# Routing, shared experts and expert blocks of a Macaron layer: another order of the first routing, an earlier table of overflow blocks, and more buffers for results and their rows

## The chip, the cores and the metric

The kernel runs on one core of a Trainium2 chip. A core has five engines that work at the same time: TensorE (PE, matrix products and transposes), VectorE (DVE), ScalarE (ACT), GpSimd (POOL) and SyncE (SP, here only a queue of DMA issues). The metric is the device time of one execution in microseconds (us); the time of a kernel is the median of its runs.

## What is computed

A layer over 4096 tokens of 256 values, all in float32: half a feed-forward, attention, half the same feed-forward again.

```python
x = x + 0.5 * ffn(layernorm(x))
x = x + attention(layernorm(x))      # 16 heads of 16 values
x = x + 0.5 * ffn(layernorm(x))

def ffn(x):
    scores = softmax(x @ Wg)                      # 32 experts
    weights, indices = top_k(scores, 4)
    y = 0
    for e in range(32):                           # at most 2048 tokens each
        y[tok] += swiglu(x[tok], W1[e], W2[e], W3[e]) * w
    return y + swiglu(x, Ws1, Ws2, Ws3)           # the shared expert
```

## The kernel before

**Stages.** The program runs six stages one after the other: `first_front` (routing and shared expert of the first feed-forward), `Layer.experts` of layer 0, `projections` (sum of the expert results, then queries, keys and values), `attention` (into which routing and shared expert of the second feed-forward are woven), `Layer.experts` of layer 1, and a last loop that sums the results.

**Order.** Inside `tc.manual_schedule(engines=ORDERED)` PE, ACT, DVE and SP work their instructions in the order in which the program writes them; only POOL's order is chosen by the framework. The order around the change is thus written out by hand, with generators: each `yield` ends a piece, and the caller decides which piece comes next. A tile with `bufs=n` has n buffers in turn; who writes a buffer again waits until its last reader is done, and what is written behind the waiting instruction on the same engine waits too.

**Routing** (`route`, L201 to L357, in chunks of 8 x 128 tokens in layer 0 and 4 x 128 in layer 1). `normalize` takes statistics on DVE (L141, L142) and writes the rows into `xr` (on ACT at L163 in layer 0, on DVE at L167 in layer 1); `turned` transposes them (L177, L180). Then gate logits (L233), softmax and top-k on DVE (L243 to L257), one-hot masks (L262 to L267), positions by a product with a triangle of ones (L273), overflow arithmetic (L281 to L332), slots (L338 to L344), and 4 indirect DMAs per 128 tokens by POOL (L350) that scatter the rows with their tags to `xg` in DRAM. Columns D + K and up of `xr` hold for each of the 4 choices the row of `ys` that the result belongs to; L222 writes them, ahead of the statistics. `xr` has 3 buffers in layer 0, for 4 chunks.

Each expert owns 512 slots; tokens beyond these go to overflow blocks of 128 rows, of which 24 are always worked (a condition works more if there are more). Which expert owns an overflow block is worked out by `share_out` (L531 to L581): transposes of the running counts `given` (L558), member tables on DVE (L561 to L566), a product (L570), and from it `eb` (the expert) and `wrow` (the row of its weights, L578), by which POOL gathers weights (L663).

**Shared expert.** `shared_half` (L410 to L453) for layer 0, 8 halves of 512 tokens: first piece 16 products (L421) and tanh (L430); second piece the gate products on DVE (L436, L437); third piece 8 products (L443), the sum (L451) and a store by SP (L452). `shared` (L359 to L408) does the same for layer 1 in smaller pieces (L375, L384 to L389, L395, L403, store L408).

**`first_front`** (L774 to L860): for each of the 4 chunks the pieces of routing, and within chunks 1 to 3 one half of the shared expert. After the last routing come the five other halves, each half's third piece after the next one's second.

**Attention** (L1136 to L1298): scores (L1170), exponentials (L1180), values (L1188), division and projection; the pieces of `front(b)` (L1240 to L1254: `route`, then `shared`) are put between steps of the next block. For the last block no step is left, so its pieces are worked one after the other at the end. PSUM is given out by `Banks`: `Banks.tile` lends always the bank that is just not the accumulator, so two tiles in a row share one bank.

**Experts** (`experts`, L502 to L529): `share_out`, then `run_blocks` (L629 to L655) over 56 blocks, 32 of 512 rows (kind "expert") and 24 of 128 (kind "more"). In round n it loads weights of block n + 4 and rows of block n + 3, turns block n + 1 (`turn`: transposes L692, copies L696 and L698, and `toi`, the target rows of the result, L700 to L709), does the first half of block n (L718, silu L727, product `hT` L729) and the second half of block n - 1 (L740, copies to `yb` L744 and L746, and 4 or 1 indirect DMAs by POOL, L748, that send the rows of `yb` to the rows of `ys` that `toi` names). `toi` has 4 buffers and `yb` the pool's 3. On DVE a round is written in the order copy, `toi`, `hT`, `yb`.

The projections hold squares of queries and keys in `sq` (L938, 7 buffers), read by L947.

Of the kernel before, what the change touches and what calls it, by code (L numbers as in the profile page):

```python
# [9 lines left out]
F32 = mybir.dt.float32  # L10
I32 = mybir.dt.int32
# [7 lines left out]
P = 128  # L19
# [40 lines left out]
def kernel(  # L60
# [122 lines left out]
    class Layer:  # L183
# [17 lines left out]
        def route(self, ch, xt, pool, pm):  # L201
# [14 lines left out]
            def over_t(a):  # L216
# [4 lines left out]
            self.xT = xT  # L221
            nc.vector.tensor_scalar(  # L222
                xr[:, :, D + K :], iota_y[:, :n, :], float(t0 * P * KR), None, ALU.add
            )
            rows = [xr[:, i, 0:D] for i in range(n)]
# [27 lines left out]
            for t in range(n):  # L253
                nc.vector.max(top[:, t, :], sc[:, t, :])
                nc.vector.max_index(idx[:, t, :], top[:, t, :], sc[:, t, :])
            idxf = xr[:, :, D : D + K]
            nc.vector.tensor_copy(idxf, idx[:, :, 0:K])  # L257
# [244 lines left out]
        def experts(self, low=None):  # L502
            if low is not None:
                few = nc.values_load(low[0:1, 0:1], min_val=0, max_val=1)
                with tc.If(few > 0), tc.tile_pool(name="low", bufs=1) as pool:
                    self.clear_low(pool)
            with (
                tc.tile_pool(name=f"expert{self.index}", bufs=3, reuse_waits="tile") as pool,
                tc.tile_pool(name=f"ps_t{self.index}", bufs=2, space=PSUM) as ps_t,
                tc.tile_pool(name=f"ps_h{self.index}", bufs=4, space=PSUM) as ps_h,  # L510
                tc.tile_pool(name=f"ps_o{self.index}", bufs=2, space=PSUM) as ps_o,
            ):
                ps = (ps_t, ps_h, ps_o)
                self.wrow = pool.tile([P, NOVMAX], I32, name="wrow", bufs=1)
                self.eb = pool.tile([P, NOVMAX], F32, name="eb", bufs=1)
                more = pool.tile([P, 1], I32, name="more", bufs=1)
                with tc.manual_schedule(engines=ORDERED):
                    halves = self.share_out(pool, ps_t, more)
                    blocks = []
                    for e in range(E):  # L520
                        blocks.append(("expert", e))
                        blocks += [
                            ("more", b) for b in range(e * NOV // E, (e + 1) * NOV // E)
                        ]
                    self.run_blocks(blocks, pool, ps)
                    large = nc.values_load(more[0:1, 0:1], min_val=0, max_val=1)
                    with tc.If(large > 0):
                        self.clear_rest(pool, ps_t, halves)
                        self.run_blocks([("more", b) for b in range(NOV, NOVMAX)], pool, ps)  # L529

        def share_out(self, pool, ps_t, more):  # L531

            def tile(n, name, dtype=F32):
                return pool.tile([P, n], dtype, tag=name, name=name, bufs=1)

            nc.vector.tensor_scalar(more[:], self.total[:], float(NOV), None, ALU.is_gt)

            whole = tile(1, "whole", I32)  # L540
            nc.vector.tensor_copy(whole[:], iota_p[:])
            nc.vector.tensor_scalar(
                whole[:], whole[:], E.bit_length() - 1, None, ALU.arith_shift_right
            )
            mod = tile(1, "mod")
            nc.vector.tensor_copy(mod[:], whole[:])
            nc.vector.tensor_scalar(mod[:], mod[:], -float(E), iota_p[:], ALU.mult, ALU.add)
            expert_of = tile(P, "expert_of")
            nc.vector.tensor_scalar(expert_of[:], ones[:], mod[:], None, ALU.mult)

            halves = []
            nch = P // E
            for h in range(self.nch // nch):
                columns = tile(3, f"columns{h}")
                for i in range(3):
                    tp = ps_t.tile([P, P], F32, tag="tp", name="given_ps")
                    part = self.given[:, i, h * nch : (h + 1) * nch, :]
                    nc.tensor.transpose(tp[:], part.rearrange("p c e -> p (c e)"), ident[:])  # L558
                    nc.vector.tensor_copy(columns[:, i : i + 1], tp[:, 0:1])
                end = tile(1, f"end{h}")  # L560
                nc.vector.tensor_add(end[:], columns[:, 0:1], columns[:, 1:2])  # L561
                member = tile(NOVMAX, f"member{h}")
                inside = tile(NOVMAX, f"inside{h}")
                nc.vector.tensor_scalar(member[:], iota_b[:], columns[:, 0:1], None, ALU.is_ge)
                nc.vector.tensor_scalar(inside[:], iota_b[:], end[:], None, ALU.is_lt)
                nc.vector.tensor_mul(member[:], member[:], inside[:])  # L566
                halves.append((member, columns))
            ps = ps_t.tile([P, NOVMAX], F32, tag="tp", name="eb_ps")
            for h, (member, _) in enumerate(halves):
# [10 lines left out]
            )  # L580
            return halves  # L581

# [88 lines left out]
        def load_rows(self, kind, i, pool):  # L671
            if kind == "expert":
                n, r, e = S0 // P, i * S0, float(i)
            else:
# [3 lines left out]

            nc.sync.dma_start(
                xb[:], self.xg[r : r + n * P, :].rearrange("(p i) d -> p i d", p=P)  # L680
            )
            return {"n": n, "r": r, "e": e, "xb": xb}

        def turn(self, b, pool, ps_t):
# [19 lines left out]
            nc.vector.tensor_reduce(to[:, :n], pair[:, :n], AX.X, ALU.add)  # L704
            toi = pool.tile([P, S0 // P], I32, tag="toi", name="toi", bufs=4)
            slot = iota_s[:] if n > 1 else iota_p[:]
# [25 lines left out]
        def second_half(self, b, pool, ps_o):  # L732
            w2, hT, n = b["w"][:, 2 * NC * H :], b["hT"], b["n"]
            yb = pool.tile([P, S0 // P, D], F32, tag="yb", name="yb")
            group = f"send{self.index}"
# [38 lines left out]
    def first_front(layer, keep):  # L774
        n = layer.n
        with (
# [57 lines left out]

            half = halves()
            norm(0)
            go_on(0, turns)
            norm(1)
            for ch in range(nch):
                go_on(ch, 1)  # L840
                if ch + 1 < nch:
                    go_on(ch + 1, turns)
                go_on(ch, 2)
                between = next(half) if ch > 0 else iter(())
                next(between, None)
                go_on(ch, 3)
                next(between, None)
                if ch + 2 < nch:
                    norm(ch + 2)
                next(between, None)  # L850
            flag = layer.low(keep)

            late = iter(())
            for it in half:
                next(it)
                next(it)
                next(late, None)
                late = it
            next(late, None)
        return flag  # L860

    def projections(layer, side):
# [4 lines left out]
        with (  # L867
# [48 lines left out]
            def queries_or_keys(c, i, xT):  # L916

                squares = []
                for g in range(NG):
# [16 lines left out]
                    if i == 0:  # L936
                        nc.scalar.dma_start(qd[c, g], part)
                    sq = pool.tile([P, QB], F32, tag="sq", name="sq", bufs=2 * NG - 1)  # L938
                    nc.scalar.activation(sq[:], ps[:], AF.Square, bias=bias)
# [195 lines left out]

    def attention(layer, kT, v, shift):  # L1136

# [4 lines left out]
        with (  # L1142
# [97 lines left out]
            def front(b):  # L1240
# [8 lines left out]
                def both():  # L1249
                    xt = xs[b]  # L1250
                    yield from layer.route(b, xt, pool, pm)
                    yield from layer.shared(b, xt, layer.xT, pool, pm)

# [79 lines left out]
    with tc.tile_pool(name="keep0", bufs=1) as keep:  # L1333
# [5 lines left out]
        with tc.tile_pool(name="kv", bufs=1, side="right", reuse_waits="tile") as kv:  # L1339
# [6 lines left out]
            layer = Layer(1, side, QT, nc.vector.tensor_copy)  # L1346
            attention(layer, kT, v, shift)
    layer.experts()
# [75 lines left out]
```

## Time and profile before

| | us |
|---|---|
| median of 3 runs (lowest to highest) | 3372.26 (3371.22 to 3374.43) |
| the profiled execution | 3374.66 |
| its span (first to last instruction) | 3372.8 |
| first front, to the last DVE sum | 0 to 229.1 |
| experts of layer 0, PE's first to last product | 236.6 to 491.4 |
| sums and projections | 502 to 707 |
| attention with the second front | 707 to 3024 |
| experts of layer 1, PE's first to last product | 3033.6 to 3292.2 |
| last sums and stores | 3302 to 3372.8 |

In lines of the profile, PE is the matrix engine, PEld its weight loads, `DVEq`, `SPq` and the like an engine's queue. A line of the timeline has the start, the duration, engine and line of the program, the operation, what it writes and reads, how many are merged, and in brackets the idle time of the engine before it with what ended it. A line of waits has who waited for whom, then the sum in us, the number of times and the longest. The granted clock is the share of full speed that PE had.

### The profile page before, as it was taken

The page shows a single profiled execution, that of the slowest core. Times are in us where ns is not written, and L with a number is a line of the kernel's source. Part 1 is how long each engine was busy: PE and PEld are TensorE (multiplying, and loading weights), DVE is VectorE, ACT ScalarE, POOL GpSimd, SP SyncE. Part 2 cuts the span into 40 slices and gives each one's busy share as a digit, 9 for nine tenths or more (in the row PEclk, how much of TensorE's full clock was granted, in tenths as well). Part 3 has the DMA queues.
Part 4 walks back from the last instruction along what each step waited for, and adds up shares of the span by engine and source line. Part 5 has one row for each costly group of instructions (what it writes and reads, how often), then busy time and mean ns, then how long its engine had stood idle before and what let it go on. Part 6 is the DMA issues. An engine that isn't in the chain of part 4 may idle for free.

```text
span 3372.8 us, 50148 instructions
## 1 busy us (share of the span) xinstructions
PE 3072.7 (91%) x20183; PEld 1066.8 (32%) x20183; DVE 975.3 (29%) x2837; ACT 2334.9 (69%) x3753; POOL 616.0 (18%) x644
## 2 busy tenths in 40 slices
PE   4589977989999999999999999999999999959990
PEld 3356653422222222222222222222222222226660
DVE  6744437810112103201211210220121131044447
ACT  2112224569999898898999989889989998912220
POOL 2756661100001000100100010010010001025661
PEclk9799998989999999999999999999999999969995
DMA  6347756441300000000000010000000000017767
GB/s 236 118 182 244 247 189 242 153 135 56 100 4 20 26 7 4 27 20 4 30 20 4 13 33 4 7 27 20 4 30 20 4 6 31 1 64 238 254 204 315
DMA packets 130352, 282.20 MB, mean 84 GB/s; under 512 B 23472, under 2 KB 70192, under 8 KB 129712
## 3 DMA queue, kind: packets, MB, share of 16 engines
q1 hardware_dynamic: 82976, 165.84, 14.6%
q0 software_dynamic: 31872, 97.56, 7.9%
q10 hardware_dynamic: 15248, 15.38, 1.3%
q8 instruction: 163, 2.67, 0.3%
q14 instruction: 93, 0.76, 0.1%
HBM read 146.64 MB, written 132.06 MB: 83 GB/s over the span
## 4 chain that ended last, share of the span: by engine, by line
PE 70%; DVE 3%; issue 2%; DMA 2%; POOL 1%; ACT 0%; DVEq 0%; POOLq 0%; SPq 0%
PE banks L1170 33%; PE banks L1188 30%; PE banks L375 2%; DMA ys<-yb,toi 2%; PE h L718 2%; DVE xt L765 1%; POOL ys L748 1%; PE banks L1260 1%; PE banks L395 1%; PE o L740 1%; PE banks L233 1%; PE xbt_ps L692 0%; PE banks L177 0%; POOL wb L663 0%; DVE hT L729 0%
## 5 line engine op out<-in xcount | busy, mean ns | idle before, releaser
L1180 ACT ACTIVATE ex<-banks 128x512 f32<-128x512 f32 (+1 forms) x3223 | 2055.7, 714 | 164.7 <-PE banks L1170 129.1
L1170 PE MATMUL banks<-q,kT 32*128 32x512 f32 x8192 | 1177.6, 641 | 12.4 <-DVE q L1157 11.1
L1188 PE MATMUL banks<-ex,v 128*17 128x512 f32 x8192 | 1078.9, 598 | 0.0
L350 POOL DMA_INDIRECT xg<-xr,sidx x256 | 248.2, 969 | 2282.3 <-DVE beyond L343 2163.4
L1170 PEld LDWEIGHTS banks<-q,kT 32*128 32x128 f32 x8192 | 327.4, 183 | 847.4 <-ACT ex L1180 704.5
L1188 PEld LDWEIGHTS banks<-ex,v 128*17 128x17 f32 x8192 | 136.1, 95 | 777.5 <-issue 776.5
L1208 DVE COPY o<-banks 128x512 f32<-128x512 f32 x32 | 22.1, 691 | 1185.4 <-PE banks L1188 647.2
L748 POOL DMA_INDIRECT ys<-yb,toi x304 | 293.0, 964 | 177.3 <-DVE yb L746 94.8
L718 PE MATMUL h<-xT,w 128*128 128x512 f32 x512 | 236.0, 604 | 0.0
L744 ACT COPY yb<-o 128x512 f32<-128x512 f32 x64 | 37.5, 586 | 178.8 <-PE o L740 153.0
L740 PE MATMUL o<-w,hT 128*128 128x256 f32 x512 | 126.7, 392 | 34.2 <-DVE hT L729 34.2
L698 ACT COPY xT<-xbt_ps 128x512 f32<-128x512 f32 (+1 forms) x112 | 50.6, 452 | 126.4 <-PE xbt_ps L692 124.8
L727 ACT ACTIVATE s<-h 128x512 f32<-128x512 f32 (+1 forms) x112 | 51.5, 460 | 107.0 <-PE h L718 105.4
L718 PEld LDWEIGHTS h<-xT,w 128*128 128x128 f32 x512 | 95.2, 196 | 95.2 <-issue 95.2
L922 PE MATMUL qk_ps<-xT,wqk_sb 128*128 128x512 f32 x256 | 113.5, 602 | 1.7 <-ACT xT L180 1.7
L740 PEld LDWEIGHTS o<-w,hT 128*128 128x128 f32 x512 | 95.4, 194 | 55.1 <-DVE hT L729 36.9
L1211 DVE RECIPROCAL den<-den 128x512 f32<-128x512 f32 x32 | 107.3, 3353 | 1.1
L765 DVE SCALAR_TENSOR_TENSOR xt<-y,wk,xt 128x256 f32<-128x256 f32 x192 | 95.1, 495 | 6.9
L729 DVE TENSOR_TENSOR hT<-s,h 128x512 f32<-128x512 f32 (+1 forms) x112 | 57.8, 516 | 74.9 <-PE h L718 71.7
L375 PE MATMUL banks<-xT,ws_sb 128*128 128x512 f32 x128 | 68.9, 664 | 8.6 <-DVE u L385 6.5
L692 PE MATMUL xbt_ps<-ident,xb 128*128 128x128 f32 x512 | 69.6, 282 | 7.7 <-DMA xb<-xg 7.7
L443 PE MATMUL so<-ws_sb,shT 128*128 128x256 f32 x128 | 36.2, 441 | 43.5 <-DVE shT L437 28.9
(215 smaller groups left out, 1781.2 us busy)
## 6 DMA issues: line engine op xcount, KB each, us to landing
y<-ys SPq DMA_DIRECT2D x64, 640.0 KB, 6.9
xb<-xg SPq DMA_DIRECT2D x64, 528.0 KB, 5.7
w<-in_wexp_dram SPq DMA_DIRECT2D x64, 384.0 KB, 3.4
xg<-zeros SPq DMA_DIRECT2D x152, 132.0 KB, 2.3
xg<-zero SPq DMA_DIRECT2D x32, 264.0 KB, 4.3
qd<-q ACTq DMA_DIRECT2D x32, 256.0 KB, 5.5
q<-qd SPq DMA_DIRECT2D x32, 256.0 KB, 2.6
xbb<-xg SPq DMA_DIRECT2D x48, 132.0 KB, 3.7
```

The source lines that it names most:

```text
L350: ins = nc.gpsimd.indirect_dma_start(out=self.xg[:], out_offset=bass.IndirectOffsetOnAxis(ap=self.sidx[:, t0 + t, k : k + 1], axis=0), in_ ...
L375: nc.tensor.matmul(ps[:], ws13_sb[:, c, h0 : h0 + P], xT[:, c, i0 * P : (i0 + QT) * P], start=(c == 0), stop=(c == NC - 1),)
L692: nc.tensor.transpose(tp[:, i * P : (i + 1) * P], xb[:, i, c * P : (c + 1) * P], ident[:])
L718: nc.tensor.matmul(ps[:, : n * P], w[:, (j * NC + c) * H : (j * NC + c + 1) * H], xT[:, c, : n * P], start=(c == 0), stop=(c == NC - 1),)
L740: nc.tensor.matmul(o[:, i, :], hT[:, (i0 + i) * P : (i0 + i + 1) * P], w2, start=True, stop=True)
L748: ins = nc.gpsimd.indirect_dma_start(out=ys[:], out_offset=bass.IndirectOffsetOnAxis(ap=b["toi"][:, i : i + 1], axis=0), in_=yb[:, i, :], ...
L765: nc.vector.scalar_tensor_tensor(xt, y[:, k, :], self.wk[:, t, k : k + 1], y[:, K, :] if k == 0 else xt, ALU.mult, ALU.add,)
L922: nc.tensor.matmul(ps[:], wqk_sb[:, cc, (i * NG + g) * P : (i * NG + g + 1) * P], xT[:, cc, :], start=(cc == 0), stop=(cc == NC - 1),)
L1170: nc.tensor.matmul(pm.all[:, banks[j], :], kT[rows, g, t * P : (t + 1) * P], q[rows, :], start=True, stop=True,)
L1180: nc.scalar.activation(ex[:, i : i + n, :], pm.all[:, k : k + n, :], AF.Exp, scale=SCALE)
L1188: nc.tensor.matmul(acc[j * HP : j * HP + HV, :], v[:, t, g * HG + j, :], ex[:, j, :], start=(t == 0), stop=(t == NT - 1),)
L1211: nc.vector.reciprocal(den[:], den[:])
```

## The change

- `route` writes the constant columns of `xr` (L222) after the top-k instead of ahead of the statistics.
- `first_front` puts two halves of the shared expert into each of the chunks 1 to 3; the third piece of the second one waits in the list `late` and is worked in the next chunk, after the logits and the next chunk's transposes (`finish`). Two halves are left for the end.
- `share_out` is called at the end of `first_front`, ahead of these two halves, and in `attention` between `route` and `shared` of the last block, instead of at the start of `experts`. What must live on lies in the pools `keep0` and `side`, its PSUM tiles come from the front's pool or from `Banks`.
- The rows of the first expert block are loaded by four DMAs, one for each of the four rows of a partition.
- `toi` gets 12 buffers instead of 4, `yb` 6 instead of 3, `sq` 6 instead of 7.

```diff
@@ route
-            nc.vector.tensor_scalar(
-                xr[:, :, D + K :], iota_y[:, :n, :], float(t0 * P * KR), None, ALU.add
-            )
             rows = [xr[:, i, 0:D] for i in range(n)]
...
                 nc.vector.max_index(idx[:, t, :], top[:, t, :], sc[:, t, :])
+            nc.vector.tensor_scalar(
+                xr[:, :, D + K :], iota_y[:, :n, :], float(t0 * P * KR), None, ALU.add
+            )
@@ experts
-                    halves = self.share_out(pool, ps_t, more)
...
-        def share_out(self, pool, ps_t, more):
+        def share_out(self, pool, pm, scratch):
...
-                    tp = ps_t.tile([P, P], F32, tag="tp", name="given_ps")
+                    tp = pm.tile([P, P], F32, tag="m", name="given_ps")
...
-            ps = ps_t.tile([P, NOVMAX], F32, tag="tp", name="eb_ps")
+            ps = pm.tile([P, NOVMAX], F32, tag="m", name="eb_ps")
@@ load_rows
-            nc.sync.dma_start(
-                xb[:], self.xg[r : r + n * P, :].rearrange("(p i) d -> p i d", p=P)
-            )
+            parts = n if kind == "expert" and i == 0 else 1
+            rows = self.xg[r : r + n * P, :].rearrange("(p i) d -> p i d", p=P)
+            for a in range(0, n, n // parts):
+                part = slice(a, a + n // parts)
+                nc.sync.dma_start(xb[:, part, :], rows[:, part, :])
@@ turn
-            toi = pool.tile([P, S0 // P], I32, tag="toi", name="toi", bufs=4)
+            toi = pool.tile([P, S0 // P], I32, tag="toi", name="toi", bufs=12)
@@ second_half
-            yb = pool.tile([P, S0 // P, D], F32, tag="yb", name="yb")
+            yb = pool.tile([P, S0 // P, D], F32, tag="yb", name="yb", bufs=6)
@@ first_front
+            late = []
+
+            def finish():
+                while late:
+                    next(late.pop(0))
+
...
                     go_on(ch + 1, turns)
+                finish()
                 go_on(ch, 2)
-                between = next(half) if ch > 0 else iter(())
-                next(between, None)
+                one, two = (next(half), next(half)) if ch > 0 else (iter(()), iter(()))
+                next(one, None)
                 go_on(ch, 3)
-                next(between, None)
+                next(one, None)
+                next(two, None)
                 if ch + 2 < nch:
                     norm(ch + 2)
-                next(between, None)
+                next(one, None)
+                next(two, None)
+                if ch > 0:
+                    late.append(two)
             flag = layer.low(keep)
-
-            late = iter(())
+            layer.share_out(keep, pm, pool)
+
             for it in half:
                 next(it)
                 next(it)
-                next(late, None)
-                late = it
-            next(late, None)
+                finish()
+                late.append(it)
+            finish()
@@ projections
-                    sq = pool.tile([P, QB], F32, tag="sq", name="sq", bufs=2 * NG - 1)
+                    sq = pool.tile([P, QB], F32, tag="sq", name="sq", bufs=2 * NG - 2)
@@ attention
                     yield from layer.route(b, xt, pool, pm)
+                    if b == NQB - 1:
+                        layer.share_out(keep, pm, pool)
                     yield from layer.shared(b, xt, layer.xT, pool, pm)
```

## The prediction

> **What bounds the kernel now.** I read the page first: PE is busy 91% of the span, and in section 4 the chain is PE for 70%. But the two big PE lines (L1170, L1188) are the attention stage, which the change hardly touches, so I cut the span by stage with the table of stretches, and looked in each touched stage for the wait that ends last.
>
> ```profile
> PE 3072.7 (91%) x20183; PEld 1066.8 (32%) x20183; DVE 975.3 (29%) x2837; ACT 2334.9 (69%) x3753; POOL 616.0 (18%) x644
> ...
> 249.70:491.40 241.70, 224.33 (x1008) 153.12 (x1006) 101.71 (x320) 63.26 (x138) 160.12 (x167) 0.99 0.71 233
> 3047.60:3292.20 244.60, 227.72 (x1008) 155.33 (x1006) 101.72 (x320) 63.35 (x138) 159.35 (x166) 0.97 0.69 230
> 700.00:3000.00 2300.00, 2265.57 (x16971) 557.10 (x16972) 410.67 (x1065) 2067.98 (x3247) 108.34 (x113) 0.99 0.07 24
> ```
>
> Columns: stretch, its length, busy time of PE, PEld, DVE, ACT, POOL, granted clock, DMA share, GB/s. The first two stretches are the two expert stages from the moment their pipelines run to PE's last matmul. PE is idle there for 17.4 and 16.9 us. The waits of these stages (windows 232 to 500 and 3030 to 3310), then PE's alone, say for what:
>
> ```profile
> DVE toi L707 <- DMA ys<-yb,toi: 87.0, 32, 7.6
> ...
> PE o L740 <- DVE hT L729: 17.4, 7, 3.5
> ...
> DVE toi L707 <- DMA ys<-yb,toi: 81.1, 28, 7.3
> ...
> PE o L740 <- DVE hT L729: 16.9, 7, 3.2
> ```
>
> In the timeline one such stall reads as a chain: DVE stands at `toi` because a send still reads the old buffer, the gate product `hT` is queued behind it, and PE's `o` waits for `hT`.
>
> ```profile
> 260.94 0.16 DVE L707 SCALAR_TENSOR_TENSOR toi<-iota_p,to 128x1 int32<-128x1 f32 x1 [7.57 <-DMA ys<-yb,toi]
> 261.04 0.69 DVE L729 TENSOR_TENSOR hT<-s,h 128x512 f32<-128x512 f32 x1
> 261.79 1.99 PE L740 MATMUL o<-w,hT 128*128 128x256 f32 x8 [3.46 <-DVE hT L729]
> ```
>
> The end of the first front: POOL's last scatter starts at 220.15, but DVE's last shared part begins at 228.39, and only then come weights and rows:
>
> ```profile
> 220.15 0.96 POOL L350 DMA_INDIRECT xg<-xr,sidx  x1 [0.30 <-DMA xg<-xr,sidx]
> ...
> 228.39 0.69 DVE L451 SCALAR_TENSOR_TENSOR xt<-so,xt 128x512 f32<-128x512 f32 x1 [1.03 <-PE so L443]
> ...
> 230.94 0.81 SPq L679 DMA_DIRECT2D xb<-xg  x2
> 236.57 3.59 PE L692 MATMUL xbt_ps<-ident,xb 128*128 128x128 f32 x16 [2.73 <-DMA xb<-xg]
> ```
>
> The end of attention: the last block's first shared matmuls run beside its routing on DVE, and the rest is one serial chain to the store L408.
>
> ```profile
> 2997.31 3.78 PE L375 MATMUL banks<-xT,ws_sb 128*128 128x512 f32 x4 [1.35 <-DVE pos L286]
> ...
> 3006.17 3.78 PE L375 MATMUL banks<-xT,ws_sb 128*128 128x512 f32 x4 [5.08 <-DVE u L385]
> ...
> 3024.22 0.37 SPq L408 DMA_DIRECT2D ys<-xq  x1
> ...
> 3029.26 0.80 SPq L679 DMA_DIRECT2D xb<-xg  x2
> ```
>
> **More buffers (toi 4 to 12, yb 3 to 6): about -39 us.** Warm, a block of 512 rows costs PE 0.87 (turn) + 3.44 (h) + 1.73 (o) = 6.04 us, an overflow block of 128 rows 0.22 + 0.89 + 0.43 = 1.54. 32 and 24 of them are 230.2 us a stage, of which 218.8 fall in the stretches above. So 241.7 = 218.8 + 17.4 stall + 5.5 slow clock, and 244.6 = 218.8 + 16.9 + 8.9. What comes late next? POOL: a send or a weight gather takes a slot of 0.96 + 0.30 = 1.27 us; 172 of them follow the first send (152 sends, 20 gathers), 218 us against PE's 219. Near equal, so POOL ends, as now, some 7 us behind PE (498.2 against 491.4), and is no new bound; its backlog, now three blocks at most by the four `toi`, fits in six `yb`. Rows come early enough: the rows of block E4 are issued at 252.94 and used at 267.70. Bounds per stage: stalls gone and clock loss kept, or both gone: -17.4 to -22.9, and -16.9 to -25.7. Here a rule speaks against the upper end. The Trainium skill (TensorE: Matmul & The Clock Gate, The HAM clock gate) says that the clock halves after about 3.4 us without work; only one of these stalls is that long, so by the rule nothing is won beyond the stalls. By the row, `o` after a stall of 3.04 us at 3059.33 took 3.59 instead of 1.73 us, so shorter stalls do cost clock. I take the stalls plus about half of the clock loss, less 1 us each for waits still unseen: -19 and -20.
>
> **Front of the first layer: -8 us.** Six of eight halves instead of three run within the routing, so two instead of five are left behind it: 3 x 10.3 us of PE work go from the end. Does the routing get late, and with it POOL's scatters? DVE has the slots at 91.6, 135.0 and 168.6; POOL reaches these chunks at 98.8, 139.8, 180.9. A half costs DVE 4 x 0.67 + 2 x 0.65 = 4 us, and its last matmuls (`finish`) now stand ahead of the top-k with 3.6 us on PE. Against that, the statistics no longer wait in chunk 3: L222 stood 5.07 us at 100.10 for an old scatter, and that wait now falls on ACT, which has time. Chunk 2 I work out at 134 us, chunk 3 at 170: both before POOL. PE and DVE then end near 211 to 214, share_out's 4.8 us (229.64 to 234.5 now) included, and POOL's 128 slots end as now at 220 to 221. Rows wait for the last scatter to land: 219.7 + 2.4 (median landing) = 222.1, or by the second layer (3024.31 to 3029.26) 4.9 us, 224.6. I take 223.4, against 230.94. Moving the constant L222 is worth 0.3 us at the start and otherwise changes the place only.
>
> Splitting the first rows into four: three more issues of 0.35 us on SP, with the second block's rows queued behind. By the rows, 528 KB land in 5.7 and 132 KB in 3.7 us, so the first part is 2 us early; by the skill (DMA: Bandwidth & Descriptors, Anatomy of one DMA; its fit of 2.0 us + bytes / 436e3, an estimate since it is for POOL's path) 3.2 and 2.3 us, 0.9 early, and its Rules for kernel authors ask to coalesce. But PE's loop is over the halves of a row outside, the four parts inside, so xT needs all four: -1 to +1, taken as -0.5. Sum: -7.5 - 0.5 = -8, bounds -6 to -10.
>
> **share_out in the last attention block: +8 us.** It is written between `route` and `shared`. On PE its six transposes stand ahead of L375, and each takes the one lent bank: transpose, DVE copy, transpose. DVE copies only after L344 ends at 3005.52. From there: five small ops 1.2, six rounds of about 0.6, two member groups of 0.85, product 0.5, two copies 0.3 each: the bank is free at about 3012.0. L375 then pays 3.8 + 0.65 + 0.7 that routing hid. From its second group the chain took 18.0 us (3006.17 to 3024.22); one of the later groups will be warm (2.0 instead of 3.8). L408 comes at 3033.5 to 3035, 9 to 11 late. Removed behind it: the wait for the scatter, 1.6 us, and the block's own share_out, which already lay beside the loads. Weights, then rows, follow L408 on SP, so PE starts 8 late (bounds +5, +17 if all of L375 and L395 stay cold). Without the scatter's landing as cover it would be +10.
>
> **Costed at nothing:** `sq` 7 to 6 buffers: the last square of a chunk waits 0.29 us for L947 already; now the seventh waits too, 0.7 us, behind 3.72 us of L961 on PE before anyone needs it. If that cover goes, 8 x 0.7 = 5.6. The L222 move in attention lies in DVE's idle time.
>
> **Sum** against the profiled execution, 3374.66 us (span 3372.8 and 1.9 around it, which stays): -19 - 20 - 8 + 8 = -39, so 3335.7. That execution is 2.4 above the median of the runs; from the median, 3333.3. I give 3334.
>
> **Rivals.**
> *The stall changes its name.* With `toi` free, DVE or ACT wait at `yb`, or PE for rows, since the DMA engines are busy 0.71 and get 8% more per us. For it: sends land in 2.4 to 7.5 us. Against it: margins of 14 us above. Half of the gain lost: 3334 + 20 = 3354.
> *The routing is late.* If PE's lower clock there (0.71 to 0.81) stretches each half's chain, POOL starves and the front wins nothing: 3342.
> *Slower: the tail decides.* PE works share_out first, all shared groups stay cold, +17; it decides once the buffers and the front together give back less than that. That is so if sends are limited by the DMA engines, so the freed buffers only lengthen their queue (0), and front gives -6: 3372 + 11 = 3383. Against it: POOL has 31 us without a slot between 249.1 and 498.2 (249 less 218), waiting for `yb` from DVE, so the sends are starved, not slow.
>
> **Chances.** Forecast 0.70, stall renamed 0.16, routing late 0.10, slower 0.04. The range 3319 to 3354 takes -54 (all best bounds: 3318) nearly in and leaves out the far half of the first rival and the slower case. Measurement tells 0.2%, 6.7 us, from no change: faster 0.94, same 0.02, slower 0.04.
>
> **What would show it.** PE's wait at L740 near 0 in both expert stages and no `toi` wait; PE's stretch there 221 to 225 us; `xb` issued at 222 to 225 right behind the last scatter; scatters still without gaps from 57 on; L408 some 73 us after the last L1188 (2960.9) instead of 63, with no L375 beside the routing. Wrong, if waits at `yb` or for `wb` of over 5 us a stage appear, or gaps between scatters.

## The result and the profile after

The changed kernel takes 3322.49 us (median of 4 runs, 3320.82 to 3325.61) against 3371.74 us (4 runs, 3370.77 to 3374.43) on the same chip: ratio 0.985, 95% interval 0.9835 to 0.9864. The profiled execution took 3322.82 us, its span is 3321.1.

The two expert stages come first, in the table of stretches of the kernel after (from the first product of an overflow block to PE's last product; columns as before). In both, PE is busy for the whole stretch, at full clock:

```profile
243.35:462.00 218.65, 218.65 (x1007) 150.87 (x1006) 104.30 (x320) 62.81 (x138) 160.36 (x167) 1.00 0.77 258
3023.05:3242.20 219.15, 219.15 (x1008) 150.97 (x1006) 104.41 (x320) 63.26 (x138) 160.28 (x167) 1.00 0.78 257
```

The waits of the first of these stages (window 222 to 500) now read the other way round. Where PE waited for DVE's `hT`, DVE waits for PE; a wait of DVE at `toi` for a send no longer exists:

```profile
DVE hT L731 <- PE h L720: 78.5, 32, 2.7
...
PE xbt_ps L694 <- DMA xb<-xg: 20.8, 5, 16.3
...
ACT yb L746 <- DMA ys<-yb,toi: 9.5, 5, 1.9
```

In the timeline, the place of the stall shown before is now one unbroken row of PE work: `o` of L742 starts where `h` of L720 ends, in 1.89 us for its merged line.

```profile
258.51 1.06 PE L720 MATMUL h<-xT,wb 128*128 128x128 f32 x8
259.41 1.89 PE L742 MATMUL o<-w,hT 128*128 128x256 f32 x8
261.14 1.04 PE L694 MATMUL xbt_ps<-ident,xb 128*128 128x128 f32 x8
```

At the front two things changed that the timeline shows at its two ends. DVE's first statistic (L141) starts at 3.84 instead of 13.36, and with it POOL's scatters start at 52.18 instead of 57.54. At the end, the rows of the first block are issued 4.5 us behind the start of the last scatter, and PE gets the four parts one by one:

```profile
3.84 0.43 DVE L141 BATCH_NORM_STATS2 st<-xt 128x6 f32<-128x256 f32 x1 [0.32 <-DMA xt<-in_x_dram]
...
214.72 0.96 POOL L350 DMA_INDIRECT xg<-xr,sidx  x1 [0.30 <-DMA xg<-xr,sidx]
...
218.19 0.82 SPq L661 DMA_DIRECT2D w<-in_wexp_dram  x2
219.23 2.49 SPq L683 DMA_DIRECT2D xb<-xg  x5
...
223.20 0.48 PE L694 MATMUL xbt_ps<-ident,xb 128*128 128x128 f32 x1 [16.28 <-DMA xb<-xg]
225.54 0.47 PE L694 MATMUL xbt_ps<-ident,xb 128*128 128x128 f32 x1 [1.86 <-DMA xb<-xg]
226.81 0.48 PE L694 MATMUL xbt_ps<-ident,xb 128*128 128x128 f32 x1 [0.80 <-DMA xb<-xg]
228.23 1.33 PE L694 MATMUL xbt_ps<-ident,xb 128*128 128x128 f32 x5 [0.94 <-DMA xb<-xg]
```

At the end of attention (PE's waits, window 2900 to 3310), share_out's transposes stand where the first group of L375 ran beside the routing. After its first transpose PE waits 8.9 us, until DVE is done with the routing and makes the first copy; the other four waits are about 0.3 us each. The first group of L375 then starts 53.0 us after the start of the last value products (2928.22 to 2981.26) instead of 39.7 (2957.64 to 2997.31); only the later groups come closer behind DVE, 1.4 us instead of 5.1.

```profile
PE banks L558 <- DVE columns L559: 10.0, 5, 8.9
...
PE banks L375 <- DVE u L385: 2.8, 2, 1.4
```

The account of the span, by landmarks that both traces have:

| stretch | before, us | after, us | difference |
|---|---|---|---|
| start to first overflow product of layer 0 | 249.69 | 243.35 | -6.3 |
| from there to the last send of layer 0 | 247.54 | 223.74 | -23.8 |
| to the first query load of attention | 210.06 | 211.02 | +1.0 |
| to the start of attention's last merged L1188 (after: L1201) | 2250.35 | 2250.11 | -0.2 |
| to the first overflow product of layer 1 | 90.01 | 94.83 | +4.8 |
| to the last send of layer 1 | 251.76 | 224.83 | -26.9 |
| to the end | 73.39 | 73.22 | -0.2 |
| span | 3372.8 | 3321.1 | -51.7 |

How well do such landmarks repeat? In a second trace of the changed kernel (run 9 below) the span was 3322.2, the first overflow product came 0.6 us earlier and that of layer 1 1.2 us later. In one run below whose front is that of the kernel before, the same landmark came 2.4 us later than before. So a single difference below some 2.5 us says little.

### The profile page after: what moved, and what is told of

Its sections match the earlier page's. It is cut to its first block, busy times and chain, and to the rows that moved or that the text cites. A ratio compares the mean times of both kernels' runs of the same rounds, so it can differ in the third digit from the quotient of the medians.

```text
span 3321.1 us, 50114 instructions
## 1 busy us (share of the span) xinstructions
PE 3061.0 (92%) x20183; PEld 1060.6 (32%) x20183; DVE 979.0 (29%) x2837; ACT 2334.0 (70%) x3753; POOL 615.0 (19%) x644
## 4 chain that ended last, share of the span: by engine, by line
PE 76%; DVE 3%; issue 1%; DMA 0%; SPq 0%; POOL 0%; ACT 0%; DVEq 0%; POOLq 0%
PE banks L1183 33%; PE banks L1201 30%; PE h L720 4%; PE o L742 2%; PE banks L375 2%; DVE xt L767 2%; PE xbt_ps L694 1%; PE banks L1275 1%; PE banks L395 1%; PE banks L230 1%; PE banks L177 0%; PE banks L273 0%; DMA xb<-xg 0%; DMA y<-ys 0%; DVE den L1224 0%
## 5 line engine op out<-in xcount | busy, mean ns | idle before, releaser
L1183 PE MATMUL banks<-q,kT 32*128 32x512 f32 x8192 | 1178.3, 641 | 11.2 <-DVE q L1170 9.9
L1201 PE MATMUL banks<-ex,v 128*17 128x512 f32 x8192 | 1079.2, 598 | 0.0
L1201 PEld LDWEIGHTS banks<-ex,v 128*17 128x17 f32 x8192 | 136.1, 95 | 778.1 <-issue 777.1
L720 PE MATMUL h<-xT,w 128*128 128x512 f32 x512 | 232.1, 596 | 0.0
L720 PEld LDWEIGHTS h<-xT,w 128*128 128x128 f32 x512 | 93.2, 192 | 92.8 <-issue 92.8
L742 PE MATMUL o<-w,hT 128*128 128x256 f32 x512 | 121.1, 379 | 0.0
L742 PEld LDWEIGHTS o<-w,hT 128*128 128x128 f32 x512 | 93.6, 190 | 17.5 <-issue 7.7
L698 DVE COPY xT<-xbt_ps 128x512 f32<-128x512 f32 (+1 forms) x112 | 58.1, 518 | 82.2 <-PE xbt_ps L694 61.6
L694 PEld LDWEIGHTS xbt_ps<-ident,xb 128*128 128x128 f32 x512 | 62.3, 145 | 37.0 <-issue 25.0
```

What stands on the lines that cost most here:

```text
L694: nc.tensor.transpose(tp[:, i * P : (i + 1) * P], xb[:, i, c * P : (c + 1) * P], ident[:])
L720: nc.tensor.matmul(ps[:, : n * P], w[:, (j * NC + c) * H : (j * NC + c + 1) * H], xT[:, c, : n * P], start=(c == 0), stop=(c == NC - 1),)
L742: nc.tensor.matmul(o[:, i, :], hT[:, (i0 + i) * P : (i0 + i + 1) * P], w2, start=True, stop=True)
L1183: nc.tensor.matmul(pm.all[:, banks[j], :], kT[rows, g, t * P : (t + 1) * P], q[rows, :], start=True, stop=True,)
L1201: nc.tensor.matmul(acc[j * HP : j * HP + HV, :], v[:, t, g * HG + j, :], ex[:, j, :], start=(t == 0), stop=(t == NT - 1),)
```

## The experiments

Each was timed beside the kernel before, in three groups; "ratio" is to that kernel in the same group. Its median was 3374.07 us in the first group (runs 1 to 4), 3374.36 in the second (runs 5 to 8) and 3376.12 in the third (runs 9 to 12).

**1. The buffers of `toi` alone, in the kernel before.**

```diff
-toi = pool.tile([P, S0 // P], I32, tag="toi", name="toi", bufs=4)
+toi = pool.tile([P, S0 // P], I32, tag="toi", name="toi", bufs=12)
```

> The kernel before with one number changed: toi 12 buffers. Theory (toi alone carries the gain, stalls and the slow clock behind them: 17.4 + 5.5 and 16.9 + 8.9 us): 3371.7 - 48.7 = 3323, and PE's stretch from the first overflow block to the last product 219 us in both expert stages. First rival (only the stalls go, the clock loss stays, and the other parts of the change bring the rest): 3371.7 - 34 = 3338. Second rival (with yb at 3 the wait moves to yb): 3350 or more, with waits for the sends at L746 or L744 on PE's path.

Measured: 3324.2 us (3323.41 to 3325.88), ratio 0.9849 (0.9836 to 0.9863). Table of stretches of this run:

```profile
252.10:470.75 218.65, 218.65 (x1007) 150.85 (x1006) 104.04 (x320) 62.82 (x138) 160.75 (x167) 1.00 0.78 258
3026.06:3245.20 219.14, 219.14 (x1008) 150.96 (x1006) 103.97 (x320) 63.30 (x138) 160.65 (x167) 1.00 0.77 257
```

One number in one line gives the same unbroken stretches as the whole change: 48.6 of the 51.7 us of span.

**2. The whole change without it.**

```diff
-toi ... bufs=12
+toi ... bufs=4
```

> The changed kernel with toi back at 4 buffers. Theory (front and tail about cancel, so toi is nearly the whole gain): 3322.5 + 49 = 3371, with PE waiting some 17 us for hT in each expert stage. Rival (front and the six yb buffers have a part of their own): 3350 to 3360.

Measured: 3371.12 us (3363.71 to 3375.78), ratio 0.9992 (0.9984 to 1.0). DVE's old wait (window 222 to 500) and PE's behind it are back, and so are the lower clock and the longer stretch:

```profile
DVE toi L709 <- DMA ys<-yb,toi: 87.8, 33, 7.2
...
PE o L742 <- DVE hT L731: 14.9, 7, 3.1
```

```profile
242.87:481.45 238.58, 223.69 (x1006) 153.09 (x1004) 101.71 (x320) 62.75 (x137) 159.07 (x166) 0.99 0.72 236
3043.29:3288.90 245.61, 227.75 (x1008) 155.71 (x1006) 101.77 (x321) 63.27 (x138) 160.09 (x167) 0.97 0.70 229
```

Everything else in the change, together and with the stalls kept, is worth 3 us by the medians, and 0 to 5.4 by the interval. Runs 1 and 2 settle the main question, from both sides.

**3. `yb` back to the pool's 3 buffers.**

```diff
-yb = pool.tile([P, S0 // P, D], F32, tag="yb", name="yb", bufs=6)
+yb = pool.tile([P, S0 // P, D], F32, tag="yb", name="yb")
```

> The changed kernel with yb back at 3 buffers. Theory (POOL lags by fewer than three blocks, so three buffers are enough): 3322.5, no change within 2 us. Rival (POOL runs so near to PE that a fourth block waits): 3330 or more, with DVE or ACT waiting at yb for sends and PE behind them.

Measured: 3322.7 us (3322.09 to 3325.21), ratio 0.9846 (0.9833 to 0.986). DVE does wait at `yb` for sends (window 222 to 500), in small pieces, and PE's stretch is the same to 0.03 us:

```profile
DVE yb L748 <- DMA ys<-yb,toi: 8.9, 8, 1.5
```

```profile
244.38:463.00 218.62, 218.62 (x1007) 150.81 (x1006) 103.68 (x320) 62.73 (x138) 160.37 (x167) 1.00 0.78 258
```

The three more `yb` buffers bring nothing. Sums of waits are not time: 8.9 us in pieces of up to 1.5 fit into DVE's slack, 87 us in pieces of up to 7.6 did not.

**4. share_out of layer 1 back at the start of the experts.**

```diff
@@ attention
-                    if b == NQB - 1:
-                        layer.share_out(keep, pm, pool)
@@ experts
                 with tc.manual_schedule(engines=ORDERED):
+                    if self.index == 1:
+                        self.share_out(pool, ps_t, pool, "tp")
...
```

> The changed kernel with layer 1's share_out back at the start of its expert stage. Theory (put between route and shared it costs what the trace shows from the last attention product to the first overflow block, +4.8): 3322.5 - 5 = 3317.5, with L408 some 8 us earlier. Rival (its place costs nothing in the end, since the rows then wait for the last scatter and for the overflow table's gathers beside them): 3322.

Measured: 3319.56 us (3319.11 to 3322.52), ratio 0.9839 (0.9825 to 0.9852), span 3317.5. From the start of the last value products (2928.84) the store L408 comes after 63.2 us instead of 74.3 (2928.22 to 3002.51; before the change 66.6), and the overflow product of layer 1 another 27.6 later instead of 20.5: a net gain of 4.0. The median gains 3 us, with intervals that overlap. The other traces decide: from the last value products to the overflow product, the ten with share_out in the last attention block need 94.3 to 97.2 us, the four with it at the start of the experts (before, runs 1, 4 and 10) 89.9 to 90.8. So the new place is worse than the old one, by about what the table above shows (+4.8).

**5. The constant L222 back ahead of the statistics.**

```diff
             self.xT = xT
+            nc.vector.tensor_scalar(
+                xr[:, :, D + K :], iota_y[:, :n, :], float(t0 * P * KR), None, ALU.add
+            )
...
-            nc.vector.tensor_scalar(
-                xr[:, :, D + K :], iota_y[:, :n, :], float(t0 * P * KR), None, ALU.add
-            )
             idxf = xr[:, :, D : D + K]
```

> The changed kernel with the constant columns (L222 of before) written ahead of the statistics again. Theory (DVE's first statistics then wait until POOL has made the constants, at 13 us instead of 3.8, and POOL's first scatter and with it its last start 5 us later): 3322.5 + 5 = 3327.5, first scatter at 57.5. Rival (the start is regained because the rows then land in a calmer moment): 3323.

Measured: 3329.96 us (3328.12 to 3331.05), ratio 0.987 (0.9852 to 0.9888). In the timeline of this run DVE stands at L222 again for POOL's `iota_y`, with the statistics queued behind:

```profile
12.71 0.18 DVE L222 TENSOR_SCALAR xr<-iota_y 128x32 f32<-128x32 f32 x1 [0.22 <-POOL iota_y L102]
12.80 0.42 DVE L141 BATCH_NORM_STATS2 st<-xt 128x6 f32<-128x256 f32 x1
```

The first scatter is back at 56.97, the last at 220.13, and the overflow product at 249.14, 5.8 us later than with the change. So this small move is one of the two parts of the front's gain.

**6. Rows of a block issued ahead of its weights.**

```diff
-            for i in range(ahead):
-                weights(i)
             for i in range(ahead - 1):
+                made.append({})
                 rows(i)
+                made[i].update(self.load_weights(*blocks[i], pool))
+            weights(ahead - 1)
```

> The changed kernel, each expert stage loading the rows of blocks 0 and 1 ahead of the weights of the same block (weights 0 and 1 together were first). Theory (at the stage's start 0.8 MB of weights share the DMA engines with the rows, at some 400 GB/s 2 us): PE's first transposes 2 us earlier in both stages, 3322.5 - 3 = 3319. Rival (h needs the weights too, so the first product comes when both are there): 3322.5, with the wait moved from the transposes to h.

Measured: 3320.8 us (3318.81 to 3322.18), ratio 0.9842 (0.9827 to 0.9857), span 3317.0. First overflow product at 240.00, 3.4 us earlier than with the change. In layer 1 nothing was gained: PE's first transposes come 3.7 us after L408 instead of 6.0, but the second block's rows and then a slower first `h` (5.34 us instead of 3.86) take it back, and the stretch from the last value products to the overflow product is 96.9 us, against 94.8 and 97.1 in the two traces of the changed kernel. The rest of the gain in the span stands where the edit gives no reason for it: between the last send of layer 0 and the first query load, 207.4 us instead of 211.0.

**7. Two buffers instead of four for the gathered overflow weights.**

```diff
-w = pool.tile([P, 2 * NC * H + D], F32, tag=tag, name=tag, bufs=4)
+w = pool.tile([P, 2 * NC * H + D], F32, tag=tag, name=tag, bufs=4 if kind == "expert" else 2)
```

> The changed kernel with 2 buffers instead of 4 for the gathered weights of overflow blocks. Theory (POOL gathers four of them, 1.5 MB, right behind the last scatter, in the moment in which the first rows load; with two buffers half of that is put off): the first rows land 2 us earlier in layer 0, 3322.5 - 2 = 3320.5. Rival (a gather that comes later makes PE wait for weights of an overflow block): 3325 or more, with waits for wb on PE.

Measured: 3328.04 us (3326.43 to 3332.74), ratio 0.9868 (0.9849 to 0.9887). With two of the four first gathers (L663) taken out of the burst of loads, the overflow product came at 240.52, 2.8 earlier. But PE's stretch is then 3.3 us longer, since PE waits for weights within it; the waits and the stretch of this run:

```profile
PE h L720 <- DMA wb<-in_wexp_dram,wrow: 2.6, 3, 1.3
```

```profile
240.52:462.50 221.98, 219.34 (x1007) 150.83 (x1005) 104.59 (x320) 62.75 (x137) 161.36 (x168) 1.00 0.78 257
```

So the four gathers seem to crowd the first rows (one trace), and the four buffers are needed later: a loss.

**8. The first rows in one DMA instead of four.**

```diff
-parts = n if kind == "expert" and i == 0 else 1
+parts = 1
```

> The changed kernel with the first block's rows in one DMA again. Theory (PE's loop needs all four parts before its first half-row is whole, and four issues push back the second block's rows; by the trace parts landed 4.0, 6.3, 7.6 and 9.0 us after the issue): 3322.5 - 1. Rival (the parts let PE work while the rest lands): 3322.5 + 1 or 2.

Measured: 3321.72 us (3317.4 to 3323.24), ratio 0.9845 (0.983 to 0.986), span 3315.7. In the timeline all four parts are there at 226.04, with 6.7 us from the issue at 219.35, where the last of four parts needed 9.0 (219.23 to 228.23):

```profile
226.04 1.97 PE L694 MATMUL xbt_ps<-ident,xb 128*128 128x128 f32 x8 [20.87 <-DMA xb<-xg]
...
230.06 3.60 PE L720 MATMUL h<-xT,w 128*128 128x512 f32 x8
```

The first overflow product came at 239.75, 3.6 earlier. Only 2.1 of this is the start of the first `h`. The other 1.5 is its duration, at a granted clock of 1.00; in the kernel after it ran at 0.70:

```profile
232.16 5.10 PE L720 MATMUL h<-xT,w 128*128 128x512 f32 x8
```

That part is not tied to the split: in run 9, with it, the first `h` took 3.68 us, but started 2.9 later than here. The six other traces whose rows come split behind the weights, with six halves in the routing, do not come near this run either: from the first issue of rows to the overflow product they need 23.7 to 25.2 us, the kernel after 24.1, this run 20.4. The median shows less than that. In the profiles, at least, the split costs time and does not save any.

**9. The changed kernel again, to compare runs 10 to 12 with (the control).**

> The changed kernel itself, unchanged, beside the three runs below, so that differences of a few us can be told. Expected by all theories: 3322 to 3323 us, ratio to the kernel before 0.985, both expert stages without a stall of PE (218.7 and 219.2 us busy in as many).

Measured: 3324.19 us (3322.17 to 3325.35), ratio 0.9845 (0.9832 to 0.9858), span 3322.2; first overflow product 242.71, that of layer 1 3024.28.

**10. Edits 4, 6 and 8 together, in the changed kernel.**

> The changed kernel with three edits together: share_out of layer 1 back at the start of the expert stage, rows of a block issued ahead of its weights, and the first rows in one DMA. Alone, these gave spans of 3317.5, 3317.0 and 3315.7 us against 3321.1. Theory (three separate causes: sum of the gains is 3.6 + 4.1 + 5.4): span 3308, time 3309 to 3311. Rival (row order and single DMA both cure the same thing, the rows landing late in the burst of loads, so one of them counts once): span about 3312, time 3313 to 3316, first h of layer 0 at about 230 us as with either alone.

Measured: 3311.6 us (3309.5 to 3315.64), ratio 0.981 (0.9797 to 0.9823), span 3309.4: 12.6 us faster than the control, with an interval that lies clear of the control's. This version beats both kernels. The timeline of its front:

```profile
221.85 1.97 PE L697 MATMUL xbt_ps<-ident,xb 128*128 128x128 f32 x8 [15.13 <-DMA xb<-xg]
226.94 1.94 PE L697 MATMUL xbt_ps<-ident,xb 128*128 128x128 f32 x8 [3.12 <-DMA xb<-xg]
228.68 4.99 PE L723 MATMUL h<-xT,w 128*128 128x512 f32 x8
```

The first rows are there 3.7 us after their issue (218.18), but PE's order puts the rows of the second block ahead of the first `h`, and these come at 226.94. The first `h` then starts 1.4 us earlier than in run 8, but takes 4.99 us instead of 3.60, at a granted clock of 0.72 instead of 1.00, and ends at the same time. So the overflow product comes at 239.76, no earlier than with either edit alone: in layer 0 the two count once, as the rival said. The whole still comes near what the theory added up (3309 to 3311), but from other places. Against the control the front gives 3.0 us, projections and attention 2.5 (for which no edit has a reason; run 6 had it too), and the stretch from the last value products to the overflow product of layer 1 gives 7.2 (97.1 to 89.9). Run 4 alone has 90.8 there, so nearly all of the 7.2 is its edit, with the control at the upper end of its kind; rows ahead of weights add 0.9 at most, and gave nothing there in run 6.

**11. The earlier order of the first front: one half per chunk, five behind, the rest of the change kept.**

```diff
-                one, two = (next(half), next(half)) if ch > 0 else (iter(()), iter(()))
+                between = next(half) if ch > 0 else iter(())
```

with the other lines of that loop put back likewise, and share_out ahead of the five halves.

> The changed kernel with the earlier order of the first front: one half of the shared expert per chunk, five behind the last routing, share_out ahead of these five. Buffers, the moved constant L222 and the rest stay. Theory (the six halves within the routing are what brings the first front's end forward): rows are issued about 12 us later than the last scatter, PE's first overflow product comes 6 us later than 243.4, time 3328 to 3331. Rival (nearly all of the front's gain came from the earlier first scatter, since rows that are issued early land late in the burst of loads): rows issued at 225 to 226, landing 5 us later, first overflow product at 243 to 245, time 3322 to 3325.

Measured: 3327.14 us (3324.67 to 3328.39), ratio 0.9853 (0.9838 to 0.9868). The last scatter starts at 214.84 and the rows are issued 11.5 us later, at 226.36; the overflow product comes at 248.00, 5.3 us later than the control's. So the six halves within the routing do have their own part, close to the theory's 6. The rival's premise, that rows issued later land faster, held: all four parts were there 5.9 us after their first issue (232.28) instead of 9.0 (10.9 in the control), and the second block's rows after 8.8 (235.18) instead of 11.2. But the rows were issued 7.1 us later than in the kernel after, so its conclusion fell.

**12. How many buffers `toi` needs.**

```diff
-toi ... bufs=12
+toi ... bufs=6
```

> The changed kernel with 6 instead of 12 buffers for toi, to find how many are needed. With 4, DVE waited 87.8 us for the sends of old toi in the first expert stage, 2.7 us each, and PE 14.9. Theory (what is short is buffers for the sends under way, by about one block of 512 rows, whose four sends take 5 us on POOL and land 2.4 to 7.5 us later, beside an overflow block or two): two more buffers are at least 7.6 us of PE's work, more than the wait of 2.7, so PE's stall is gone: 3322 to 3326. Rival (the sends' backlog fills whatever is given, so that DVE waits again at the sixth): PE still loses 5 or more us a stage, 3332 to 3350.

Measured: 3323.44 us (3321.94 to 3324.18), ratio 0.9842 (0.9828 to 0.9855). Table of stretches:

```profile
244.35:463.00 218.65, 218.65 (x1007) 150.85 (x1006) 104.86 (x320) 62.88 (x138) 160.84 (x167) 1.00 0.77 258
3023.81:3242.96 219.15, 219.15 (x1008) 150.96 (x1006) 104.82 (x320) 63.31 (x138) 160.68 (x167) 1.00 0.78 257
```

Six are as good as twelve. DVE waited 33 times at four buffers, 2.7 us each on average, and two more buffers put the reuse two blocks later, at least 7.6 us of PE's work (6.04 + 1.54) where one of them has 512 rows. DVE no longer waits at `toi` for a send: the backlog does not fill what it is given.

## Why the prediction was right, and where its sum was off

Direction and size were right: -49 us by the medians against -39 forecast, the mechanism the one it named. Its terms, against the table of landmarks:

**The buffers: -50.7 measured, -39 forecast; the mechanism right, the term for the slow clock mis-sized.** The computed floor of 218.8 us a stage was exact (218.65 and 219.15). Both stages went to the far bounds that the prediction gave, -22.9 and -25.7: PE's stretches shrank by 23.1 and 25.5. The prediction took half of the clock's share (5.5 and 8.9) and 1 us a stage for waits unseen. All of the former came back, and none of the latter appeared. The evidence for the higher value was in the trace of before, since PE was busy 224.33 and 227.72 us for work that takes 218.8 at full clock, and that excess came only with stalls. It is not all clock, though: by the lines of the last section about 1.8 us a stage are the restarts behind the stalls, and 3.6 and 6.9 the lowered clock. The comparison of 3.59 with 1.73 us overstates it a little: as a line of the timeline an unbroken `o` takes 1.89. The rest, 0.8 and 1.5 us, is the last sends, now closer behind PE. Waits at `yb` of more than 5 us a stage, which the prediction had named as a sign of its failure, are there (9.5 us above). They were a bad sign to choose: they stand on ACT, in pieces of at most 1.9 us, and PE does not wait for them.

**`toi` or `yb`?** The prediction costed the two as one edit. Runs 1, 3 and 12 part them: `toi` from 4 to 6 gives the whole gain of the expert stages, `yb` nothing that can be told.

**The front: -6.3 measured, -8 forecast, as a sum of three errors.** L222 was costed at 0.3 us, "worth 0.3 us at the start". This looked at its idle time in brackets (0.22) and not at what stood before it: DVE's next statistic could start at 3.84. It was worth 5.8 (run 5). The halves brought the issue of the rows 7.1 us forward (run 11), near the forecast 7.5, but the overflow product only 5.3. The landing of the rows was taken as in the kernel before (5.6 us from issue to PE), but took 9.0, among the weights and gathers that start beside them (5.4, 7.3 and 5.9 in runs 6, 7 and 11, where fewer of these start with them). The split was costed at -0.5 with bounds of 1 either way; it is +3.6 in the profile (run 8), 2.1 of it a later first `h` and 1.5 a slower one, which not every trace with the split shows. These add up to -7.5; the landmark says -6.3, -7.0 in the control. That this lies within the bounds of -6 to -10 is luck: one term was 5.5 us too small and two were too favourable by 2.2 and 4.1.

**share_out at the end of attention: +4.8 measured, +8 forecast.** The chain was followed rightly: L408 came 71.1 us after the end of the last value products instead of 63.3 (forecast 73 instead of 63), and no L375 ran beside the routing. The gap from L408 to the overflow product shrank by 2.9 us (23.4 to 20.5) where 2 was taken. So the term erred by 2 at the store and 1 behind it. At the store, share_out was sized well but added wrongly: its items give 7.6 us and not the 6.5 that lead to 3012.0, and 6.8 were measured (2974.45 to 2981.26). What made the store earlier was that DVE's routing ended 46.2 us after the start of the last value products instead of 47.9.

**Costed at nothing.** `sq` shows nowhere: the stretch that holds it changed by +1.0 us, within what repeats. The sends of layer 0 do land later behind the last one, and the sum's first load is issued 7.8 us after its end instead of 3.8 (at 475.82, before at 501.99); ACT's weight loads are issued ahead of it, which may be what gives most of this back (not tried apart).

**The rivals.** "The stall changes its name" fell, as no stretch of PE holds a wait. "The routing is late" fell: the scatters run from 52.18 to 214.72 us in 162.5 us, before in 162.6. The slower rival fell with the buffers; its other half, the tail, is real at a third of its price.

## What to carry to other kernels

The table of offsets of an indirect send is held until the send has landed, as long as the data (here DVE's 87.0 us at `toi`), so it wants as many buffers as the sends under way: count both, and look in the waits for the one that stands ahead of somebody else's work on its engine. Where stalls of a few us sit in a stage, compare its busy time with the same instructions in an unbroken stretch; what is over is restarts and lost clock, and here it came back in full with the stalls. And before a constant is costed at its own duration, ask what it waits for and what stands behind it: a 0.18 us instruction held the start of the kernel by 9.5 us here, of which 5.4 reached the first scatter.

## What was not expected of the hardware

**Some stalls of 2.0 to 3.2 us cost clock, and the longest of all did not.** Seven stalls a stage, 17 us in sum, made the same 1008 products take 224.33 and 227.72 us instead of 218.65 and 219.15, at a granted clock of 0.99 and 0.97 instead of 1.00; run 2 repeats it (223.69 and 227.75). Lines of the first stage before:

```profile
292.96 2.42 PE L740 MATMUL o<-w,hT 128*128 128x256 f32 x8 [2.12 <-DVE hT L729]
...
295.60 4.70 PE L718 MATMUL h<-xT,w 128*128 128x512 f32 x8
...
325.93 1.99 PE L740 MATMUL o<-w,hT 128*128 128x256 f32 x8 [2.24 <-DVE hT L729]
...
388.51 2.40 PE L740 MATMUL o<-w,hT 128*128 128x256 f32 x8 [2.68 <-DVE hT L729]
...
453.35 1.99 PE L740 MATMUL o<-w,hT 128*128 128x256 f32 x8 [3.01 <-DVE hT L729]
```

In the unbroken stages of the kernel after, `o` takes 1.89 us and `h` 3.60. Behind eight of the fourteen stalls `o` took 1.99: that is the restart alone, at a granted clock of 1.00. Together with the 0.16 us by which an unbroken `o` overlaps the line ahead of it, a restart costs about 0.26 (an estimate from these lines), 1.8 in seven. Behind the other six (2.12 and 2.68 us long in the first stage; 3.04, 2.03, 2.40 and 3.16 in the second) `o` took 2.40 to 3.59 at a clock of 0.55 to 0.80, and behind five of these the next `h` still took 4.37 to 4.72 at 0.76 to 0.82. What these lines and the transposes between them took beyond 1.99, 3.60 and 0.38 us is 3.6 and 6.9 us, the lost clock.

The Trainium skill (TensorE: Matmul & The Clock Gate, The HAM clock gate) names about 3.4 us without work as the point at which the clock halves. Of the kernel before only the longest stall reaches that (3.46 us, the one shown ahead of the result), and `o` behind it took 1.99 at a clock of 1.00; of run 2 none does (longest 3.1 and 3.0 us). So by the rule next to nothing should have been lost beyond the stalls; here the measurement decides. The length of the stall alone does not tell which ones cost clock (2.03 us did, 2.17 and 3.01 did not), and why stays open.

**A load split in four landed later than the whole.** The stretches of the kernel after show the granted clock, the share of the DMA engines that was busy and the rate in the last three columns:

```profile
218.00:223.00 5.00, 0.00 (x0) 0.00 (x0) 0.00 (x0) 0.00 (x0) 3.22 (x4) 0.50 0.78 230
223.00:228.00 5.00, 1.43 (x3) 0.55 (x3) 0.00 (x0) 0.00 (x0) 0.61 (x1) 0.50 0.99 368
228.00:233.00 5.00, 3.90 (x14) 3.03 (x15) 1.69 (x5) 2.01 (x3) 0.00 (x0) 0.50 1.02 397
```

Two weights, the rows, and POOL's four gathers all start within 5 us; the four parts reached PE 4.0, 6.3, 7.6 and 9.0 us after the first issue, the whole in 6.7 (run 8, one trace). In all seven traces with four parts behind the first two weights and six halves in the routing, the last part needed 7.7 to 10.9. Ahead of the weights the same four parts were there in 5.4 (run 6) and the whole in 3.7 (run 10). Whether it is the smaller packets or the later issue of the last parts was not told apart.
